# Statistics, bias rows, a PSUM bank and paces in a two-layer attention and convolution kernel

## The chip, the cores and the metric

The kernel runs on one core of a Trainium2 chip. A core has TensorE (PE, matrix products; PEld is its loading of weights), VectorE (DVE), ScalarE (ACT), GpSimd (POOL) and SyncE (SP, here only issuing DMAs), which run beside one another and wait for each other by semaphores. SBUF is the working memory; PSUM holds the results of TensorE[...]. Time is measured on the device in microseconds (us); less is better. Before the change it was 2578.98 us, the median of three runs from 2576.24 to 2585.12.

## What is computed

Two layers on x of 2 x 56 x 56 positions with 384 channels, all in float32. Layer 0 is neighbourhood attention with an MLP; layer 1 is a depthwise convolution with four scans and an MLP.

```python
# layer 0
h = neighborhood_attention(layer_norm(x, ln1_g, ln1_b), w_qkv, b_qkv, rpb, w_proj, b_proj, 12, 7)
x = x + h                                   # x1
y = layer_norm(x, ln2_g, ln2_b)
x = x + gelu(y @ w1 + b1) @ w2 + b2         # x2; w1 is 384 x 1536, w2 is 1536 x 384
# layer 1
p = layer_norm(x, n1_g, n1_b) @ w_in + b_in           # 768 channels
local = depthwise_conv3x3(p, k_conv)
mixed = 0.25 * (lr + rl + tb + bt) + local            # four exponential scans of local
x = x + (layer_norm(mixed, on_g, on_b) @ w_out + b_out)     # x3
x = x + gelu(layer_norm(x, n2_g, n2_b) @ w1 + b1) @ w2 + b2
```

## The kernel before

All 6272 tokens are worked in tiles of 128 and groups of four tiles. The order in which each engine gets its instructions is the order of the program text: it is written by hand[...].

1. Attention, up to about 669 us. It writes x1 to DRAM.
2. MLP of layer 0, groups 0 (one tile) to 12 (`groups`). While group g is in the MLP, the group before it, `waiting`, is normalised and goes through `project_in` (w_in), whose result p is stored to DRAM. Groups 1 to 4 (`EARLY`) use products with fewer multiplications: `hidden_by_seven` (block sums of w1 and of the input, so that seven products do the work of eight) and `tokens_by_seven`. Group 5 uses the first of the two; from group 6 on the plain forms `hidden` and `tokens` run.
3. Convolution and scans, from about 1015 to 1917 us. This is side work for VectorE, ScalarE and DMAs beside TensorE's products. The class `Beside` plans it: `go(worth, own)` is called after every piece of main work, adds `rate * worth - own` to a budget and issues side steps (each with its own estimate in us) until the budget is used up. `MLP` is worth 2.6, `OUT` 3.9, `ROW` 7.8; `own` counts VectorE's statistics in that piece. `until(job)` issues all steps up to a job at once. `Band` jobs do the taps (L1304) and horizontal scans (L1250, L1254), `Columns` jobs the vertical scans, with turning copies on ACT (L1352, L1370). Results are added to `mix_d` in DRAM by POOL's accumulating DMAs (L1323).
4. Layer 1's out projection and MLP, groups `dgroups`. `project_out` is called once for group 0 and then in each iteration of the loop over the first three groups (`switch = 3`), where the plain products run; from there on the seven-product forms come back with other PSUM pools (`open_banks`) and weight sums, called the switch below.

Names that matter here:

- `Norm.add` is VectorE's statistics of one tile (L221, L222), `close` (L226, and POOL's power L229) and `shift` (L250) turn them into scale and offset, `apply_by_scalar` (L257) applies them on ACT. `close_by_pool` (L236 to L239) is the form in which POOL also makes the offset.
- `statistics_ahead` (L1547 to L1565) loads tiles of x1 two by two and measures them for the groups from 6 on; each `next(statistics)` is one pair.
- `hidden_by_seven` makes for each of three units u the block sums L1670 (needed before TensorE may go on accumulating in `z[u]`) and, later, L1642. Its argument `measuring` is advanced twice in each unit: here it is the generator `both()`, which in each advance runs `ahead_of(m)` and `behind(m)` for two values of m. So what is written for m = 0 and 1 comes after the first product into `z[0]`, m = 2 and 3 before L1670 of unit 0, m = 4 and 5 in unit 1, and so on.
- `add_row` (L1136) adds a bias row to all tiles of a group by an accumulating DMA that POOL issues. `seeded` (L1225) copies the residual with its bias into a PSUM bank before `tokens` accumulates onto it.
- `bank()` hands out two PSUM banks in turn, `y_end` and `y`. `ps_t` has three banks, used in turn for transposes (`tp`) and for measuring (`xi`, L1440); `ps_m` has three for the MLP.
- `sums_of_w1` (L1591) makes five differences of blocks of w1: on POOL for layer 0, on VectorE at the switch for layer 1, where the first three go into a tile in the place of w_in.

Of the kernel before, what the change touches and what calls it, by code (L numbers as in the profile page):

```python
# [33 lines left out]
F32 = mybir.dt.float32  # L34
AF = mybir.ActivationFunctionType
ALU = mybir.AluOpType
# [6 lines left out]
P = 128  # L43
# [70 lines left out]
class Beside:  # L114
# [2 lines left out]

    def __init__(self):
        self.jobs, self.due, self.finished, self.idle = [], 0.0, set(), True
        self.late, self.rate, self.begun = [], 1.03, False  # L120
        self.steps = self.run()

    def behind(self, kind=object):
# [55 lines left out]
def block_kernel(ctx: ExitStack, tc: tile.TileContext, ins: dict, out: bass.AP):  # L179
# [914 lines left out]
    def passes(xs, xn, w1, w2, between=lambda ps: None):  # L1094
# [116 lines left out]
        def tokens(lhs, w, k, ps=None, onto=None):  # L1211

            ps = onto if onto is not None else bank() if ps is None else ps
            for m, t in enumerate(lhs):
                nc.tensor.matmul(  # L1215
                    ps, lhsT=t[:, k * P : (k + 1) * P], rhs=w[:, m, :],
                    start=m == 0 and onto is None, stop=m == len(lhs) - 1,
                    skip_group_check=onto is not None,
                )
            return ps  # L1220
# [251 lines left out]
                return 2 * STATS  # L1472
            return 0.0

        def project_out(g, mx, x, inner, then=lambda k: None):
            n = dgroups[g][1]
            x3 = io.tile([P, NT, C], F32, name="xc")
            norm = Norm(sm)
            for k in range(n):
                ps = tokens([mx[:, c, :] for c in range(NI)], w_out, k)  # L1480
                nc.vector.scalar_tensor_tensor(
                    x3[:, k, :], ps, inner.rs[:, k : k + 1], x[:, k, :], ALU.mult, ALU.add
                )
                norm.add(k, [x3[:, k, :]])
                then(k)
                beside.go(OUT, 2 * STATS)
            norm.close(n)
            return x3, norm
# [88 lines left out]
            for k in tiles:  # L1577
                yield from measure_by_vector(ahead[0], ahead[2], k)

        def sums_of_w1(w1, three, engine=nc.gpsimd):  # L1580

            h = HID // 2
            b11, b12 = w1[:, 0, :h], w1[:, 0, h:]
            b21, b22 = w1[:, 1, :h], w1[:, 1, h:]
            t1, t2, t3 = (three[:, c, :] for c in range(NC))
            t4, other = (tp.tile([P, h], F32, name=x) for x in ("w1_t4", "w1_other"))
            for to, x, y in (
                (t1, b12, b11), (t2, b22, t1), (t3, b22, b12), (t4, b21, t2),
                (other, w1[:, 2, :h], w1[:, 2, h:]),
            ):  # L1590
                engine.tensor_tensor(to, x, y, ALU.subtract)  # L1591
            return t1, t2, t3, t4, other

        def sums_of_input(hT):

# [180 lines left out]
        ps_y, ps_u, bank_b, banks_b = open_banks(fctx, "first")  # L1776
        ps_t = ps_m = ps_u
        tag = "uz"
        w1_sums = sums_of_w1(w1, tp.tile([P, NC, HID // 2], F32, name="w1_t"))
        x = xs.pop(0)  # L1780
        hT = channels(xn, groups[0][1], "L0_conv_ln2_g", "L0_conv_ln2_b")
        add_row(x, groups[0][1], "b2_0")
# [1 line left out]
        for g, (t0, n) in enumerate(groups):  # L1784
# [19 lines left out]
            if g == last:  # L1804
                beside.until((0, NI - 1))
                load_row(0, "b2_1")
                ahead = load_mix(0)
                beside.rate = 1.03
            if g < last:
                x_next, n_next = xs.pop(g + 1), groups[g + 1][1]  # L1810
                norm_next = Norm(sm) if g < EARLY.stop else Ready(g + 1)
# [22 lines left out]
            def behind(m):  # L1834

                nonlocal xn_next
                if g < last:
                    if g < EARLY.stop and 2 * m < n_next:
                        for k in range(2 * m, min(2 * m + 2, n_next)):
                            norm_next.add(k, [x_next[:, k, :]])  # L1840
                    if g < EARLY.stop and m == 1:
                        norm_next.close(n_next)
                    if g < EARLY.stop and m == 5:
                        norm_next.shift(n_next)
                    to = 7 if g < EARLY.stop else 8
                    if m == to:
                        xn_next = xp.tile([P, NT, C], F32, name="xn")
                    if to <= m < to + n_next:
                        norm_next.apply_by_scalar(m - to, x_next, xn_next)
                if m == 2 and g:  # L1850
                    add_row(x, n, "b2_0")

            def both():
                for m in range(NHID):
                    ahead_of(m)
                    behind(m)
                    if m % 2 == 0 and m > 2 and sum_steps:
                        sum_steps.pop(0)()
                    if m % 2 == 1:
                        if g > 1:  # L1860
                            next(statistics, None)
                        yield

            if early or half_early:
                s12 = [tp.tile([P, NHID // 2, MT // 2], F32, name=x) for x in ("s1", "s2")] if early else None
                low, high, finish = hidden_by_seven(
                    hT, xsums, w1, w1_sums, s12, both(), "L0_conv_b1"
                )
                hT_w = io.tile([P, NC, MT], F32, name="hT")
                nw = groups[waiting[0]][1]  # L1870
                to_channels(
                    None, [xn_w[:, k, :] for k in range(nw)], hT_w, NC, *n1,
                    banks=[
                        ps_y.tile([P, MT], F32, name="turn", tag="y"), y_end_wide,
                        ps_u.tile([P, MT], F32, name="turn", tag="ua", bufs=1),
                    ],
                )
                if half_early:
                    finish()
                    hid = [t[:, i] for t in (*low, *high) for i in range(2)]  # L1880
                    begin_convolution()
                    seeds = [seeded(x, k) for k in range(2)]
                    project_in(waiting[0], hT_w)
                else:
                    project_in(waiting[0], hT_w, finish, 0)
            else:
                for m in range(NHID):
                    next(preparing, None)
                    ahead_of(m)
                    hid.append(hidden(w1, m, hT, n, "L0_conv_b1"))  # L1890
                    behind(m)
                    if g > EARLY.stop and m in (8, 10):
                        seeds.append(seeded(x, m // 2 - 4))
                    own = STATS if m == 1 else 0.0
                    if g == last:
                        own = measure_beside(m, 0, ahead)
                    beside.go(MLP, own)
                for _ in preparing:
                    pass
                if g == 0:  # L1900
                    between(bank())
                if waiting is not None:
                    project_in(waiting[0], hT_w)
            if g == last:
                ahead[2].close(dgroups[0][1])
                w1, w2_1, w_parts = weights(1)
                for part in w_parts[:3]:
                    part()
# [67 lines left out]
        add_row(x3, dgroups[0][1], "b2_1")  # L1976
        for g, (t0, n) in enumerate(dgroups[:switch]):
            hid = []
            for m in range(NHID):
                hid.append(hidden(w1, m, hT, n, "L1_conv_b1"))  # L1980
                beside.go(MLP, measure_beside(m, g + 1, ahead))
            res = x3
            x3, norm = project_out(g + 1, *ahead)
            ahead = load_mix(g + 2)
            seeds = [seeded(res, k) for k in range(2)]
            for k in range(n):
                if g == switch - 1 and k == 2:

                    beside.until((1, NI - 1))
                    cctx.close()  # L1990
                    tp = pctx.enter_context(tc.tile_pool(name="tail", bufs=1, reuse_waits="tile"))
                    three = wp.tile([P, NC, INNER], F32, name="w1_t", tag="w_in")
                    w1_sums = sums_of_w1(w1, three, nc.vector)
                    w2_sums, sum_steps = sums_of_w2(w2, nc.vector)
                if k == n - 1:
                    hT = channels(xn, dgroups[g + 1][1], *n2)
                ps = tokens(hid, w2, k, onto=seeds.pop(0))
                if k == 0:
                    norm.shift(dgroups[g + 1][1])
                if k == n - 3:  # L2000
                    xn = normalized(norm, x3, dgroups[g + 1][1])
                beside.go(ROW)
                if k == n - 1:
                    add_row(x3, dgroups[g + 1][1], "b2_1")
                o = res[:, k, :]
                nc.scalar.copy(o, ps)
                nc.sync.dma_start(out=yout[t0 + k * P : t0 + (k + 1) * P, :], in_=o)
                if k + 2 < n:
                    seeds.append(seeded(res, k + 2))
# [146 lines left out]
```

## Time and profile before

One execution was profiled: it took 2580.42 us, of which the profile's span is 2578.6 us. TensorE's mean granted clock was 0.995.

| stage (us from the span's start) | TensorE | VectorE | ScalarE | POOL | DMA share |
|---|---|---|---|---|---|
| 835 to 855, MLP of layer 0, group 3 | 15.91 | 11.43 | 10.73 | 6.04 | 0.61 |
| 1415 to 1435, group 10 | 15.59 | 11.88 | 13.47 | 0.00 | 0.45 |
| 1640 to 1660, project_out of group 0 | 17.43 | 19.41 | 6.58 | 2.15 | 0.44 |
| 1656 to 1920, layer 1 up to the switch | 262.56 | 238.60 | 139.98 | 39.07 | 0.78 |
| 1915 to 1935, the switch | 15.32 | 19.70 | 8.90 | 9.17 | 0.91 |

The numbers are us of busy time of each engine in that stretch; a stretch of 20 us with TensorE at 15.91 has 4.09 us in which TensorE did nothing. In the first, second and last of them TensorE's granted clock was 0.83, 0.83 and 0.91, elsewhere 1.00.

### The profile page before, as it was taken

How to read it: one execution, taken by the hardware profiler on the slowest of the kernel's cores; microseconds unless marked ns; L12 is line 12 of the kernel's file. 1: busy time of each engine (PE TensorE's matmuls, PEld its weight loads, DVE VectorE, ACT ScalarE, POOL GpSimd, SP SyncE). 2: the span in 40 equal slices, each digit the busy share in tenths (PEclk: the TensorE clock that was granted, in tenths of full speed). 3: DMA queues.
4: the chain of work that ended last, by engine and by line, in shares of the span. 5: the costliest groups of instructions: out<-in, count | busy, mean ns of one | idle time of the engine just before them, and what ended most of it. 6: DMA issues, size and time to landing. Idle time of an engine off the chain costs nothing. (4 is left out here: it accounts for less than half of the span.)

```text
span 2578.6 us, 41862 instructions
## 1 busy us (share of the span) xinstructions
PE 2537.1 (98%) x16678; PEld 1737.8 (67%) x16678; DVE 1978.9 (77%) x3718; ACT 1123.9 (44%) x2033; POOL 569.0 (22%) x615
## 2 busy tenths in 40 slices
PE   9999999999999999999999999999999999999999
PEld 5666666666688777455445555555558888888888
DVE  4888978887454453799999898799897877878871
ACT  5665655655443444334444443323762233333222
POOL 0111211111542231110110011011133333333332
PEclk9999999999999999999999999999999999999999
DMA  7423454225521322657677566776881333333210
GB/s 229 152 88 98 159 179 155 83 90 192 145 67 57 86 68 63 171 169 217 174 221 265 191 187 187 246 207 151 235 202 46 74 74 74 74 74 74 47 28 21
DMA packets 155596, 342.96 MB, mean 133 GB/s; under 512 B 11158, under 2 KB 109696, under 8 KB 153088
## 3 DMA queue, kind: packets, MB, share of 16 engines
q1 hardware_dynamic: 124096, 255.65, 29.2%
q0 software_dynamic: 26352, 57.81, 13.2%
q10 hardware_dynamic: 4944, 26.74, 3.1%
q8 instruction: 133, 2.18, 0.4%
q14 instruction: 71, 0.58, 0.1%
HBM read 176.39 MB, written 134.88 MB: 121 GB/s over the span
## 5 line engine op out<-in xcount | busy, mean ns | idle before, releaser
L1304 DVE SCALAR_TENSOR_TENSOR loc<-pt,taps,loc 128x1045 f32<-128x1045 f32 (+17 forms) x288 | 366.7, 1273 | 22.0 <-ACT loc L1287 14.2
L1197 PE MATMUL mm<-hT,w 128*128 128x512 f32 x720 | 317.7, 596 | 1.2 <-ACT hT L274 1.2
L573 ACT ACTIVATE pts<-pts 119x448 f32<-119x448 f32 (+5 forms) x396 | 210.7, 573 | 109.2 <-DVE pts L563 100.0
L563 DVE TENSOR_TENSOR pts<-sc,bias 119x448 f32<-119x448 f32 (+5 forms) x396 | 219.0, 615 | 45.4 <-PE sc L552 45.0
L1197 PEld LDWEIGHTS mm<-hT,w 128*128 128x128 f32 x720 | 135.3, 191 | 162.8 <-issue 155.9
L1180 DVE STREAM_TRANSPOSE hT<-xn 32x96 f32<-32x96 f32 x784 | 211.3, 269 | 27.7 <-ACT xn L257 17.5
L406 PE MATMUL ps<-hT,wqkv 128*128 128x448 f32 x504 | 204.8, 550 | 2.1 <-ACT vs L451 1.5
L1452 DVE STREAM_TRANSPOSE turned<-mx 32x192 f32<-32x192 f32 x528 | 194.8, 369 | 6.9
L1215 PE MATMUL y<-w,hid 128*128 128x384 f32 x552 | 181.9, 486 | 0.0
L1215 PE MATMUL y_end<-w,hid 128*128 128x384 f32 x552 | 181.8, 486 | 0.0
L1215 PEld LDWEIGHTS y_end<-w,hid 128*128 128x128 f32 x552 | 104.5, 190 | 71.8
L1215 PEld LDWEIGHTS y<-w,hid 128*128 128x128 f32 x552 | 104.3, 190 | 71.5 <-issue 0.5
L1208 ACT ACTIVATE hid<-mm,chan 128x512 f32<-128x512 f32 x120 | 82.3, 686 | 156.7 <-PE mm L1197 156.7
L406 PEld LDWEIGHTS ps<-hT,wqkv 128*128 128x128 f32 x504 | 91.3, 189 | 84.3 <-issue 74.2
L1197 PE MATMUL mm<-hT,w_in 128*128 128x512 f32 x324 | 140.8, 593 | 0.6 <-DVE hid_u L1642 0.6
L229 POOL TENSOR_TENSOR rs<-rs,mhalf 128x4 f32<-128x4 f32 (+4 forms) x60 | 58.8, 981 | 314.5 <-DVE rs L226 305.5
L1623 PE MATMUL ua<-hT,w 128*128 128x256 f32 x504 | 123.7, 382 | 0.0
L1323 POOL DMA_DIRECT2D mix_d<-both x36 | 32.7, 908 | 408.4 <-ACT both L1319 326.2
L552 PEld LDWEIGHTS sc<-qT,kT 32*100 32x100 f32 (+3 forms) x3168 | 87.8, 169 | 46.6 <-DVE sum L582 7.6
L592 PE MATMUL o<-pts,vt 100*32 100x112 f32 (+3 forms) x3168 | 116.8, 264 | 0.6 <-ACT pts L573 0.6
L1630 ACT ACTIVATE hid<-hid_u,chan 128x256 f32<-128x256 f32 x168 | 76.1, 500 | 86.4 <-DVE hid_u L1642 68.8
L1197 PEld LDWEIGHTS mm<-hT,w_in 128*128 128x128 f32 x324 | 61.2, 190 | 77.5 <-issue 73.1
(207 smaller groups left out, 4985.4 us busy)
## 6 DMA issues: line engine op xcount, KB each, us to landing
loc<-loc_d SPq DMA_DIRECT2D x24, 784.0 KB
xa<-x_d SPq DMA_DIRECT2D x24, 768.0 KB
xa<-rows POOLq DMA_DIRECT2D x24, 768.0 KB, 9.3
bias<-in_bias_t ACTq DMA_DIRECT2D x13, 1344.0 KB
p_d<-mx SPq DMA_DIRECT2D x11, 1536.0 KB
mx<-mix_d SPq DMA_DIRECT2D x11, 1536.0 KB
v_d<-vs SPq DMA_DIRECT2D x49, 192.0 KB
xr<-in_x SPq DMA_DIRECT2D x49, 192.0 KB
```

Of the source, the lines that this page charges most:

```text
L406: nc.tensor.matmul(ps, lhsT=wqkv[:, c, m * P : (m + 1) * P], rhs=hT[:, c, half_of(n)], start=c == 0, stop=c == NC - 1,)
L552: nc.tensor.matmul(sc[i // 2][: w.keys, i % 2, q : q + TT], lhsT=kT[d, hg, w.keys_at + r * w.kc : w.keys_at + (r + w.rows) * w.kc], rhs=qT ...
L563: nc.vector.tensor_tensor(self.pts[:n, h : h + 2, lo:hi, :], sc[half][:n, :, at * TT : (at + hi - lo) * TT].rearrange("p h (c q) -> p h c ...
L573: nc.scalar.activation(t, t, AF.Exp)
L592: nc.tensor.matmul(o[i * HD : (i + 1) * HD, self.slot, :TT], lhsT=w.vt[:n, c, h * HD : (h + 1) * HD], rhs=self.pts[:n, i, c, :], start=c = ...
L1180: nc.vector.transpose(hT[j : j + HD, :, k * P + i : k * P + i + HD], xn[i : i + HD, k, :].rearrange("p (c q) -> p c q", c=NC)[:, :, j : j ...
L1197: nc.tensor.matmul(ps[:, : n * P], lhsT=w[:, c, m * P : (m + 1) * P], rhs=hT[:, c, : n * P], start=c == 0, stop=c == NC - 1,)
L1208: nc.scalar.activation(t[:, : n * P], ps[:, : n * P], AF.Gelu, bias=col(b1, m))
L1215: nc.tensor.matmul(ps, lhsT=t[:, k * P : (k + 1) * P], rhs=w[:, m, :], start=m == 0 and onto is None, stop=m == len(lhs) - 1, skip_group_c ...
L1304: nc.vector.scalar_tensor_tensor(to, pt[:, lo + dy - self.top : hi + dy - self.top, xt : xt + n], self.tap(dy, dx), to, ALU.mult, ALU.add,)
L1452: nc.vector.transpose(t[j : j + HD].rearrange("p (m c) -> p m c", m=NI)[:, :, i : i + HD], mx[i : i + HD, :, k * P + j : k * P + j + HD],)
L1623: nc.tensor.matmul(bank[:, i, :], lhsT=w[:, m * P : (m + 1) * P], rhs=x, start=start and i == 0, stop=True, skip_group_check=True,)
```

## The change

- `Beside.rate` is 1.04 instead of 1.03 from the start, and 1.06 instead of 1.03 from the last group of layer 0 on.
- `project_out`, called without `then`, takes the bank for every third tile (k = 2 of four) from `ps_t` instead of from `bank()`.
- The five sums of w1 are split: `sums_of_w1` makes three, always on POOL, and `more_of_w1` the other two. For layer 1, POOL makes its three at the start of the loop's group 1; VectorE makes the other two at the switch, where it made all five.
- In groups 0 to 4 the statistics of the next group's x1 come two tiles at m = 3 and two at m = 5 instead of four at m = 0 and 1; close, shift and applies follow (m = 5, 7 and 8 instead of 1, 5 and 7). The pairs of `statistics_ahead` are taken at m = 1, 7, 9 and 11 from group 1 on, instead of at every odd m from group 2 on.
- The bias row b2_0 is added to the next group's tiles after `project_in`, instead of to the group's own tiles at m = 2.

```diff
-        self.late, self.rate, self.begun = [], 1.03, False
+        self.late, self.rate, self.begun = [], 1.04, False
...
-        def project_out(g, mx, x, inner, then=lambda k: None):
+        def project_out(g, mx, x, inner, then=None):
...
-                ps = tokens([mx[:, c, :] for c in range(NI)], w_out, k)
+                third = then is None and k % 3 == 2
+                ps = tokens(
+                    [mx[:, c, :] for c in range(NI)], w_out, k,
+                    ps_t.tile([P, C], F32, name="y", tag="pt") if third else None,
+                )
...
-                then(k)
+                if then is not None:
+                    then(k)
...
-        def sums_of_w1(w1, three, engine=nc.gpsimd):
+        def sums_of_w1(w1, three):
             h = HID // 2
             b11, b12 = w1[:, 0, :h], w1[:, 0, h:]
-            b21, b22 = w1[:, 1, :h], w1[:, 1, h:]
+            b22 = w1[:, 1, h:]
             t1, t2, t3 = (three[:, c, :] for c in range(NC))
+            for to, x, y in ((t1, b12, b11), (t2, b22, t1), (t3, b22, b12)):
+                nc.gpsimd.tensor_tensor(to, x, y, ALU.subtract)
+            return t1, t2, t3
+
+        def more_of_w1(w1, sums, engine=nc.gpsimd):
+            h = HID // 2
             t4, other = (tp.tile([P, h], F32, name=x) for x in ("w1_t4", "w1_other"))
             for to, x, y in (
-                (t1, b12, b11), (t2, b22, t1), (t3, b22, b12), (t4, b21, t2),
-                (other, w1[:, 2, :h], w1[:, 2, h:]),
+                (t4, w1[:, 1, :h], sums[1]), (other, w1[:, 2, :h], w1[:, 2, h:]),
             ):
                 engine.tensor_tensor(to, x, y, ALU.subtract)
-            return t1, t2, t3, t4, other
+            return *sums, t4, other
...
-                beside.rate = 1.03
+                beside.rate = 1.06
...
-                    if g < EARLY.stop and 2 * m < n_next:
-                        for k in range(2 * m, min(2 * m + 2, n_next)):
+                    if g < EARLY.stop and m in (3, 5):
+                        for k in range(m - 3, min(m - 1, n_next)):
                             norm_next.add(k, [x_next[:, k, :]])
-                    if g < EARLY.stop and m == 1:
+                    if g < EARLY.stop and m == 5:
                         norm_next.close(n_next)
-                    if g < EARLY.stop and m == 5:
+                    if g < EARLY.stop and m == 7:
                         norm_next.shift(n_next)
-                    to = 7 if g < EARLY.stop else 8
-                    if m == to:
+                    if m == 8:
                         xn_next = xp.tile([P, NT, C], F32, name="xn")
-                    if to <= m < to + n_next:
-                        norm_next.apply_by_scalar(m - to, x_next, xn_next)
-                if m == 2 and g:
-                    add_row(x, n, "b2_0")
+                    if 8 <= m < 8 + n_next:
+                        norm_next.apply_by_scalar(m - 8, x_next, xn_next)
...
                     if m % 2 == 1:
-                        if g > 1:
+                        if m not in (3, 5):
                             next(statistics, None)
...
                     project_in(waiting[0], hT_w)
+            if g < last:
+                add_row(x_next, n_next, "b2_0")
...
         for g, (t0, n) in enumerate(dgroups[:switch]):
             hid = []
+            if g == 1:
+                three = sums_of_w1(
+                    w1, wp.tile([P, NC, INNER], F32, name="w1_t", tag="w_in")
+                )
...
-                    three = wp.tile([P, NC, INNER], F32, name="w1_t", tag="w_in")
-                    w1_sums = sums_of_w1(w1, three, nc.vector)
+                    w1_sums = more_of_w1(w1, three, nc.vector)
```

More of the change, by code (lines that the diff above doesn't have):

```diff
@@ L1778, in passes @@
         tag = "uz"
-        w1_sums = sums_of_w1(w1, tp.tile([P, NC, HID // 2], F32, name="w1_t"))
+        w1_sums = more_of_w1(w1, sums_of_w1(w1, tp.tile([P, NC, HID // 2], F32, name="w1_t")))
         x = xs.pop(0)
```

## The prediction

> **What bounds the kernel now.** I read the busy shares first, then the waits of TensorE, then the timeline at each place where TensorE stood still.
>
> ```profile
> PE 2537.1 (98%) x16678; PEld 1737.8 (67%) x16678; DVE 1978.9 (77%) x3718; ACT 1123.9 (44%) x2033; POOL 569.0 (22%) x615
> DVE  4888978887454453799999898799897877878871
> PEclk9999999999999999999999999999999999999999
> ```
>
> TensorE is busy for 98% of the span, and no edit removes a matmul. So a gain can only come from its idle time: 2578.6 - 2537.1 = 41.5 us, plus what slow clocks cost. VectorE (DVE) is at 9 tenths in slices 17 to 30, the convolution: there it is nearly a second bound.
>
> ```profile
> PE uz L1623 <- DVE sh L250: 7.8, 3, 4.1
> PE tp L271 <- ACT xn L257: 4.7, 2, 4.4
> ...
> PE yb L1229 <- ACT hT L274: 2.7, 1, 2.7
> PE y L1215 <- DVE xc L1481: 2.6, 1, 2.6
> ...
> PE ub L1623 <- issue: 2.0, 1, 2.0
> ```
>
> These five rows (us in all, times, longest) are 19.8 us and touch the edits; the rest of the idle time lies in the attention stage and at the two ends, where nothing is edited. In order of time:
>
> ```profile
> 835.35 0.56 DVE L221 BATCH_NORM_STATS2 st<-xa 128x6 f32<-128x384 f32 x1 [4.43 <-DMA xa<-x_d]
> 840.96 0.66 DVE L1670 TENSOR_TENSOR hid_u<-uz,hid_u 128x512 f32<-128x512 f32 x1
> 841.77 2.04 PE L1623 MATMUL uz<-xsums,w 128*128 128x256 f32 x4 [4.09 <-DVE sh L250]
> 843.60 1.91 PE L1623 MATMUL uz<-hT,w 128*128 128x256 f32 x4
> ...
> 1405.28 1.33 POOL L1136 DMA_DIRECT2D xa<-rows  x1
> 1419.84 0.48 ACT L1225 COPY y<-xa 128x384 f32<-128x384 f32 x1 [6.00 <-DMA xa<-rows]
> 1422.40 2.18 PE L271 MATMUL tp<-ident,xn 128*128 128x128 f32 x9 [4.41 <-ACT xn L257]
> ...
> 1648.11 4.14 PE L1215 MATMUL y<-w_out,mx 128*128 128x384 f32 x12 [2.57 <-DVE xc L1481]
> 1656.21 0.61 DVE L1481 SCALAR_TENSOR_TENSOR xc<-y,rs,xa 128x384 f32<-128x384 f32 x1
> ...
> 1916.88 3.17 ACT L1370 ACTIVATE mixed<-line 128x392 f32<-128x392 f32 x4 [3.84 <-DVE line L1254]
> 1922.42 0.32 PE L1229 MATMUL yb<-zeros 128*128 128x384 bf16 x1 [2.69 <-ACT hT L274]
> 1930.48 0.58 ACT L1662 COPY hid_u<-ub 128x512 f32<-128x512 f32 x1 [4.76 <-DMA mix_d<-mixed]
> ```
>
> (Start, length, engine, line; in brackets the idle time before and its releaser.) A, group 3: DVE waits for x1, then does four statistics and two pairs for later groups before the block sum L1670 that TensorE needs. B, group 10: ACT waits for the bias row that POOL issued late. C: the third product of project_out waits for the first to be read. E: the side work's last scan ends late, ACT's reads of it stand before the next stage's evictions, and a transfer holds the memory that the new stage's first sum needs.
>
> [...] after the 4.09 us gap four records take 1.91 us against 1.03 elsewhere. From 841.77 to 849.07 is 7.30 us; the same work one group later takes 4.56, so 2.7 us are lost besides. After 4.41 us the loads of weights stand 0.86 apart instead of 0.43 for 5.4 us: 2.7 again. After 2.69 us it costs some 1.5; after 2.57 and 2.46 nothing. [...]
>
> ```profile
> 663.95 1.80 POOL L1591 TENSOR_TENSOR w_t<-w 128x768 f32<-128x768 f32 x1
> 664.01 1.75 DVE L250 SCALAR_TENSOR_TENSOR sh<-mv,rs 128x1 f32<-128x1 f32 x1 [1.96 <-POOL rs L229]
> ```
>
> A DVE instruction on one column takes 1.75 us beside POOL, against 0.16 elsewhere.
>
> **The change, part by part.** Against the profiled run.
>
> *Statistics (A).* The gaps on `uz` are 1.26, 4.09 and 2.45 us in groups 2 to 4, with 2.7 of slow clock and a follower of 0.28: 10.8. Before the first L1670, DVE now has one pair for later groups and two tiles of x1, each tile 0.53 + 0.18: 2.9 us instead of 5.8. In the tightest group, 3, x1 lands at 835.35, so L1670 begins at 835.35 + 1.45 = 836.8 and ends at 837.5; TensorE asks at 837.68. In groups 2 and 4 over 2 us are left. All 10.8 goes. What is late next: the normalisation moves one step down, so in groups 1 to 4 the last step on ACT has one more apply of 0.70 us before the copy L1669 and the evictions L274 that release project_in. ACT has 0.29 us free there and TensorE 0.05; I take 0.3 each, 1.2 in all (ends 0 and 4 x 0.7 = 2.8). In group 4 POOL's power of 4.80 us now comes late; its successors have over 20 us. Net gain 9.6.
>
> *Bias rows (B).* The 1.3 us issue leaves POOL's queue at m == 2, where it stood behind L238 (which waits for DVE), and goes behind project_in: some 50 us before the seeds read it, for a landing of 9.3 us (14.5 at 1405). It waits there for applies that ACT has done, and behind it stand only powers of the next group. It costs nothing, and ACT's 6.00 us go: gain 4.41 + 2.7 = 7.1. Late next is L238's own chain, which feeds an apply at 1405.41 with 0.07 us to spare; pace 1.04 puts 3.5 us more side work ahead of it. ACT has some 1.3 us free per step and TensorE three banks: I take 0 (end 1).
>
> *Third bank (C).* TensorE runs on at 1645.5. But the bank comes from the three of the transposes that follow, and the third of those needs it back: it is read at 1656.21 + 0.61, by DVE, which is full there. Project_in starts at 1657.4 as before. Gain 0.1 (ends 0 and, if the buffers fall otherwise, 2.5). Its use is in the next three calls: the first product may be read 3.9 us later.
>
> *Paces.* Walking the planner with its own costs at both paces: at the switch 3.6 us of side work are left at 1.03 and none at 1.06; priced at the trace's durations, DVE is given 4.2 us more ahead of the first statistics of the second layer's group 1, and 7.1 ahead of its group 2. It has idle time for part: in this stage it waited 2.4 us at 1694 and 3.4 and 4.3 us at 1899 and 1857 for ACT copies that now come earlier in ACT's order. The gap of 1.17 us at 1674 (an eviction behind such a copy) should mostly close: 0.8.
>
> *Sums of w1.* DVE is spared 3 x 0.95 = 2.8 us at the switch; POOL gets 3 x 1.80 at 1754, with 10 us free before its next issue. But [...] 5.4 us fall on DVE. Together with the pace it is late at the first statistics by 4.2 + 5.4 - 2.4 - 0.5 (a wait at 1716) = 6.7 us. The second pair's transposes reuse that bank: read until 1769.9, wanted at 1773.5, so 3.6 are free and TensorE stands 3.1 us (ends 0 and, with slow clock, 5.8).
>
> *Switch (E).* Gaps 2.69 and 1.99 and slow clock 1.5: 6.2. Both hang on the end of the last scan at 1916.84. Against TensorE it moves by +5.4 (POOL) - 2.9 (idle already counted) - 3.1 (TensorE's own stall), and by what it recovers of 3.6 and 8.8 us of idle time after 1769; a third of that gives -4.7. Gain 4.5 (ends 0 and 6.2). DVE's next block sum ends at 1936.06 and is spared 2.8 besides, so it isn't late next.
>
> Sum: 9.6 + 7.1 + 0.1 + 0.8 - 3.1 + 4.5 = 19.0. The profiled run took 2580.42, 1.4 above the median: 2561.4 there, **2560** for the median.
>
> **The rivals.**
> - All of it lands: no stall from POOL, C in full, E in full: 10.8 + 7.1 + 2.5 + 0.8 + 6.2 = 27.4, 2551.6. For it: DVE's waits of 4.3 and 3.4 us are for ACT alone. Against: the exclusion seen at 664.
> - DVE takes back: E brings nothing, the 5.8 falls twice and ACT costs 2.8: 8.0 + 7.1 - 11.6 = 3.5, 2575.5. For it: DVE is busy 238.6 of 264 us from 1656 on. Against: it waits for TensorE four times near 1780 to 1805.
> - x1 lands later than at 835.35 and group 3 keeps its gap: 19.0 - 6.8 = 12.2, 2566.8. For it: 0.2 us of room. Against: 4.4 us in the other groups.
> - Slower: DVE is never caught up in the second layer, and each pair of statistics there finds its bank unread. The point is a lateness of about 5.5 us (one pair every 5.8 us). [...] Against: the free 25 us of VectorE.
>
> **How the numbers follow.** Forecast 0.55, all lands 0.17, taken back 0.15, late landing 0.06, slower 0.07. The forecast's own range is 2554 to 2567; half of the first rival and most of the second come in with 2551 to 2573. What a measurement can tell here is 0.3%, 7.7 us: faster 0.55 + 0.17 + 0.06 and 0.04 of the second rival, 0.82; same 0.11; slower 0.07.
>
> **What would show it.** No wait on `uz` for L250 in groups 2 to 4, and a short one of project_in for L274 there. No 6 us wait of ACT for `xa<-rows`. At project_out 0 the wait moves from `y` to `tp`. A wait on `xi` near 1773 with DVE instructions stretched beside POOL L1591. The last scan 4 to 5 us nearer to the switch's start. I am wrong if DVE's lateness reaches several pairs, or if new ACT collisions from the shifted copies outweigh the closed one.

## The result and the profile after

The changed kernel takes 2569.35 us (median; 2563.81 to 2572.71), against 2580.1 us of the kernel before beside it: a ratio of 0.9959, interval 0.9947 to 0.9970. It is faster by 10.8 us, 0.41%, where 19.0 us were forecast. The profiled execution took 2569.35 us as well, its span 2567.6 us. The time lies just outside the forecast's own range of 2554 to 2567, on the side of the rival in which VectorE takes back (2575.5).

The same two rows of the page, busy shares and VectorE's slices, for the changed kernel:

```profile
PE 2532.3 (99%) x16676; PEld 1733.0 (67%) x16678; DVE 1986.1 (77%) x3715; ACT 1124.0 (44%) x2033; POOL 570.3 (22%) x618
...
DVE  3888878887554453899999996999877877878862
```

TensorE's idle time fell from 41.5 to 35.3 us. VectorE is busy 7.2 us longer, though three sums have left it: instructions of it that now run beside POOL are stretched. In layer 0 these are five of L250, which take 1.21 to 2.58 us (6.7 us more in all, and TensorE waits for none of them); in the second layer they are taps and a scan, shown below. The waits of TensorE in the changed kernel (us in all, times, longest); line numbers from `Beside` on are those of the new file, so L1481 is now L1485 and L1591 is L1592:

```profile
PE xi L1440 <- DVE st L221: 6.7, 2, 4.2
...
PE tp L271 <- DVE xc L1485: 2.5, 1, 2.5
...
PE uz L1197 <- ACT hT L274: 1.6, 4, 0.9
PE y L1215 <- DVE xc L1485: 1.5, 1, 1.5
...
PE y_end L1215 <- ACT y_end L1225: 1.4, 1, 1.4
```

The row `uz L1623 <- DVE sh` (7.8 us before) is gone, as are the 4.4 us at `tp <- ACT xn` and the two waits at the switch. What stands there now is in the second layer: two waits of the measuring transposes `xi` for VectorE's statistics, two at the first project_out, one for a seed.

To see where the gain is lost, the table takes the start of the same TensorE instruction in both traces as a mark, and gives the length of each stage between marks (us). The first mark is the product of one column that TensorE makes at the end of group 0, at 680.93 before and 680.72 after; the rows' times are those of the kernel before.

| stage | before | after | difference | forecast |
|---|---|---|---|---|
| 681 to 1010, MLP with block sums | 328.58 | 317.36 | -11.22 | A, -9.6 |
| 1010 to 1339, groups 6 to 9 | 329.37 | 328.89 | -0.48 | 0 |
| 1339 to 1444, group 10 | 105.29 | 98.21 | -7.08 | B, -7.1 |
| 1444 to 1583 | 139.27 | 139.56 | +0.29 | 0 |
| 1583 to 1676, first project_out and project_in | 92.17 | 94.05 | +1.88 | C and D, -0.9 |
| 1676 to 1779, first pairs of statistics | 103.30 | 110.02 | +6.72 | +3.1 |
| 1779 to 1860, pairs of the next group | 81.28 | 85.75 | +4.47 | 0 |
| 1860 to 1912, last pairs and project_out | 51.63 | 53.24 | +1.61 | 0 |
| 1912 to 1953, the switch | 40.71 | 33.65 | -7.06 | E, -4.5 |
| 1953 to the end of the span | 626.07 | 626.15 | +0.08 | 0 |

The two large gains came as forecast. What was missed is VectorE's lateness between 1583 and 1912: 14.7 us, where 2.2 were forecast. Of these, 8.6 us are more idle time of TensorE, and 5.6 us are lost because its granted clock was 0.50 behind a gap (half of its busy time at that clock; called half clock below, the prediction's slow clock). The timeline of the changed kernel shows its places (start, length, engine, line; in brackets the idle time before and its releaser):

```profile
1632.27 4.14 PE L1215 MATMUL y<-w_out,mx 128*128 128x384 f32 x12 [1.51 <-DVE xc L1485]
1639.76 1.11 PE L271 MATMUL tp<-ident,xn 128*128 128x128 f32 x4 [2.48 <-DVE xc L1485]
...
1727.54 9.82 DVE L1304 SCALAR_TENSOR_TENSOR loc<-pt,taps,loc 128x616 f32<-128x616 f32 x7
1737.39 2.92 DVE L1250 TENSOR_TENSOR_SCAN both<-decay,loc 128x616 f32<-128x616 f32 x1
...
1731.88 2.61 POOL L1592 TENSOR_TENSOR w_t<-w 128x768 f32<-128x768 f32 x1
1734.57 2.20 POOL L1592 TENSOR_TENSOR w_t<-w,w_t 128x768 f32<-128x768 f32 x1
1736.73 2.29 POOL L1592 TENSOR_TENSOR w_t<-w 128x768 f32<-128x768 f32 x1
...
1760.95 0.90 PE L1440 MATMUL xi<-ident,mx 128*128 128x128 f32 x3 [4.17 <-DVE st L221]
1761.64 7.33 PE L1197 MATMUL mm<-hT,w 128*128 128x512 f32 x12
...
1843.13 3.42 DVE L1250 TENSOR_TENSOR_SCAN line<-decay,line 128x1568 f32<-128x1568 f32 x1 [1.91 <-ACT line L1352]
1846.72 1.02 DVE L221 BATCH_NORM_STATS2 st<-xi 128x6 f32<-128x384 f32 x2
1847.33 0.68 PE L1440 MATMUL xi<-ident,mx 128*128 128x128 f32 x3 [2.56 <-DVE st L221]
...
1900.24 3.42 DVE L1254 TENSOR_TENSOR_SCAN line<-decay,line 128x1568 f32<-128x1568 f32 x1
1903.70 3.21 ACT L1370 ACTIVATE mixed<-line 128x392 f32<-128x392 f32 x4 [2.08 <-DVE line L1254]
1907.26 0.48 ACT L1225 COPY y_end<-xc 128x384 f32<-128x384 f32 x1
1907.80 8.01 PE L1215 MATMUL y_end<-w,hid 128*128 128x384 f32 x24 [1.45 <-ACT y_end L1225]
```

Beside POOL's sums seven taps take 9.82 us and a scan 2.92; elsewhere in this trace seven take 6.00 and such a scan 1.44. Some 20 us later the transposes wait 4.17 us, and the twelve products behind them take 7.33 us instead of 5.3: half clock. In the next group a scan that itself waits for a turning copy of ACT stands ahead of the pair's statistics (a pair is the two statistics instructions of one tile). At the end ACT's copies of the last scan stand ahead of a seed, for which TensorE waits 1.45 us. TensorE's granted clock (the third figure from the end of each line of the view by windows, a mean over the window, idle time included) shows that the waits cost more than their length:

```profile
1637.00:1647.00 10.00, 7.53 (x20) 3.79 (x19) 9.32 (x12) 3.26 (x5) 1.17 (x2) 0.83 0.96 318
...
1757.00:1765.00 8.00, 4.05 (x7) 2.04 (x8) 7.79 (x13) 0.45 (x1) 0.89 (x1) 0.62 0.63 161
```

### The profile page after: what moved, and what is told of

It reads as the page before. It is cut to its first block, busy times and chain, and to the rows that moved or that the text cites. A ratio compares the mean times of both kernels' runs of the same rounds, so it can differ in the third digit from the quotient of the medians.

```text
span 2567.6 us, 41855 instructions
## 1 busy us (share of the span) xinstructions
PE 2532.3 (99%) x16676; PEld 1733.0 (67%) x16678; DVE 1986.1 (77%) x3715; ACT 1124.0 (44%) x2033; POOL 570.3 (22%) x618
```

## The experiments

The theory to be tried: POOL's sums and the paces together make VectorE late, each for a part. Its rivals: the pace alone; the third bank; the new places of the statistics themselves. Each run is shown in one table, as the difference of each stage's length from the kernel before (us, between the same marks); the first stage is -11.2 in all of them, and the stages from 1010 to 1583 together are -7.3 in all. So what follows concerns the rest.

Two cautions. One execution of each kernel was profiled, and whether a gap of some 2.5 us is followed by half clock, which costs 1.7 us, differs between executions (e8 and e2 in the last section): a difference of that size in a stage with such a gap is not by itself an effect of the edit. And the part ahead of the first mark, which no experiment touches, is left out of "all": it took from some 678 to 686 us in the twelve profiled executions. The medians hold this scatter too, so they tell less than the stages.

| kernel | 1583 to 1676 | to 1779 | to 1860 | to 1912 | switch | to the end | all |
|---|---|---|---|---|---|---|---|
| changed kernel | +1.88 | +6.72 | +4.47 | +1.61 | -7.06 | +0.08 | -10.79 |
| e1, sums by VectorE | +2.04 | 0.00 | +4.92 | +1.62 | -7.10 | +0.01 | -16.98 |
| e2, paces 1.03 | -0.30 | +1.38 | 0.00 | -0.01 | -0.55 | -0.02 | -18.02 |
| e3, third bank not in the first call | +3.59 | +7.77 | +4.48 | +1.62 | -7.05 | +8.42 | +0.36 |
| e4, the three together undone | -0.10 | 0.00 | 0.00 | 0.00 | +0.86 | +8.45 | -9.30 |
| e5, sums by VectorE and paces 1.03 | -0.29 | 0.00 | 0.00 | 0.00 | +1.14 | +0.07 | -17.60 |
| e6, e5 with a bank of the MLP | -2.85 | 0.00 | 0.00 | 0.00 | -0.01 | +0.02 | -21.35 |
| e7, e6 with pace 1.15 late | -2.85 | +0.01 | 0.00 | -0.01 | -3.75 | +0.04 | -25.08 |
| e8, e2 with six sums | +1.40 | +7.35 | 0.00 | 0.00 | +1.14 | +0.05 | -8.58 |
| e9, e7 with pace 1.30 | -2.85 | 0.00 | 0.00 | +5.09 | -5.41 | -0.01 | -21.70 |
| e10, e7 with POOL's sums in group 2 | -2.85 | +0.01 | +4.35 | 0.00 | -4.60 | +0.04 | -21.58 |

**e1.** The five sums of w1 by VectorE at the switch, as before.

```diff
...
-            if g == 1:
-                three = sums_of_w1(
-                    w1, wp.tile([P, NC, INNER], F32, name="w1_t", tag="w_in")
-                )
...
-                    w1_sums = more_of_w1(w1, three, nc.vector)
+                    three = wp.tile([P, NC, INNER], F32, name="w1_t", tag="w_in")
+                    w1_sums = more_of_w1(w1, sums_of_w1(w1, three, nc.vector), nc.vector)
```

> The changed kernel, with all five sums of w1 made by VectorE at the switch as before. Theory of the lock (the three POOL sums cost VectorE 5.4 us and make it late at the statistics of the second layer): the gaps on xi of 4.17 and 2.56 us shrink to under 1.5 us together, 8 to 11 us come back in that stage, and 2 to 4 us are lost at the switch, where VectorE has 2.8 us more to do: 2560 to 2565 us. Rival (the pace alone makes it late): the gaps on xi stay above 2 us each and the time is 2569 to 2573 us.

It took 2566.03 us (ratio to before 0.9946, 0.9930 to 0.9962). The first gap on `xi` vanished, with its half clock: 6.72 us. The second did not, it grew from 2.56 to 3.29 us. And nothing came back at the switch: 2.8 us more of VectorE's work there cost nothing. So the lock (VectorE's instructions take longer beside POOL's sums, 5.3 us in all in the changed kernel) is needed for the first stall, and not for the second. The expectation held for the first gap only.

**e2.** Both paces at 1.03.

```diff
-        self.late, self.rate, self.begun = [], 1.04, False
+        self.late, self.rate, self.begun = [], 1.03, False
...
-                beside.rate = 1.06
+                beside.rate = 1.03
```

> The changed kernel with both paces at 1.03. Theory of the lock: VectorE is late by some 4 us less at the first statistics, so the first gap on xi falls from 4.17 us to about 0 to 1 and the second from 2.56 us to under 1, but 3.6 us of side work are left for the switch, where 3 to 6 us come back as idle time: 2562 to 2568 us. Rival (the pace alone): both gaps vanish and the switch stays closed, 2558 us. Rival (neither matters; the third bank or the bias rows moved it): both gaps stay, 2569 us.

2565.81 us (0.9945, 0.9929 to 0.9962). The first gap on `xi` fell to 1.16 us and the second went, so the second is the pace's; but the switch kept its two gaps (2.69 and 2.00 us). So the closed switch belongs to the pace, not to the sums. The half clock at the first project_out went too, but that is not shown to be the pace's doing: e8 is the same kernel up to there, has the same gap of 2.59 us, and lost 1.7 us. The lock can be read here without the pace. Timeline of e2:

```profile
1739.32 2.59 POOL L1592 TENSOR_TENSOR w_t<-w 128x768 f32<-128x768 f32 x1
1741.99 3.05 POOL L1592 TENSOR_TENSOR w_t<-w,w_t 128x768 f32<-128x768 f32 x1
1745.00 2.35 POOL L1592 TENSOR_TENSOR w_t<-w 128x768 f32<-128x768 f32 x1
...
1739.96 2.00 DVE L1252 SCALAR_TENSOR_TENSOR both<-both 128x11 f32<-128x11 f32 x1
1743.35 9.80 DVE L1304 SCALAR_TENSOR_TENSOR loc<-pt,taps,loc 128x605 f32<-128x605 f32 x8
...
1842.83 1.00 DVE L221 BATCH_NORM_STATS2 st<-xi 128x6 f32<-128x384 f32 x2
1848.41 3.42 DVE L1250 TENSOR_TENSOR_SCAN line<-decay,line 128x1568 f32<-128x1568 f32 x1 [4.34 <-ACT line L1352]
```

The same work without POOL beside it, in e4:

```profile
1724.67 6.86 DVE L1304 SCALAR_TENSOR_TENSOR loc<-pt,taps,loc 128x605 f32<-128x605 f32 x8
...
1733.05 0.18 DVE L1252 SCALAR_TENSOR_TENSOR both<-both 128x11 f32<-128x11 f32 x1
```

2.94 and 1.82 us: the three sums cost VectorE 4.8 us here, 5.3 in the changed kernel. The last line of e2 explains the second stall: at 1.03 the scan that waits for ACT comes after the first two pairs; at 1.06 the planner had issued it, and the scan before it, ahead of the first pair.

**e3.** The third bank in the later calls alone.

```diff
-                third = then is None and k % 3 == 2
+                third = g > 0 and then is None and k % 3 == 2
```

> The changed kernel, in which project_out of the first group takes its third bank as before and only the later calls have the new one. Theory (the bank given away is missed at once by the transposes): the gap on tp of 2.48 us goes, the gap on y grows from 1.51 to about 2.5 us, and 1.5 to 2 us are gained there, 2567.5 us; the gaps on xi move by under 1 us. Rival (VectorE's lateness of one piece of taps makes both gaps, whatever bank is used): the sum of the two stays at 4 us, 2569.4 us.

2579.93 us (1.0002, 0.9991 to 1.0012): all of the gain gone, a miss of both theories. The gap on `y` at the first project_out is 5.30 us, against 1.51 and 2.48 us with the bank, so with pace 1.04 the third bank in the first call is worth 1.3 us of gaps (1.7 in the stage) and not a loss. And there is a cost that nobody had asked for; groups of lines of e3 from 1940 to 2480, a row of the plain products after the switch:

```profile
L1726 PE MATMUL y<-w,hid 128*128 128x192 f32 x372 | 65.0, 328 | 6.2 <-DVE xc L1485 6.2
```

Eight waits of 0.78 us, one in each later group, in a stage that is 8.4 us longer; the 2.2 us besides are not placed. Four calls with a third bank make twelve calls of `bank()`, an even number; three make thirteen, and the two banks change roles for the rest of the kernel.

**e4.** The edits of e1, e2 and e3 together.

> The changed kernel with the sums by VectorE, both paces at 1.03 and no third bank in the first project_out: what is left is the order of the statistics, the bias rows and the third bank in later calls. Theory: both gaps on xi vanish, the statistics and the bias rows keep their 19 us, and the switch has its gaps of before (2.69 and 1.99 us with 1.5 of slow clock): before minus 19 to 20, 2560 to 2562 us. Rival (the statistics' or bias rows' new places themselves make VectorE late in the second layer): a gap on xi of over 2 us stays, 2566 us or more.

2570.4 us (0.9966, 0.9956 to 0.9976). No gap on `xi`: the statistics and bias rows do not make VectorE late in the second layer. The switch has two gaps as before (2.65 and 3.08 us), and the turned banks cost 8.45 us, which is why the time is no better than the changed kernel's.

**e5.** The edits of e1 and e2, so e4 with the third bank in all calls.

> The changed kernel with the sums by VectorE and both paces at 1.03, but with the third bank in all calls of project_out; it differs from the run with three parts undone in the first call's bank alone. Theory (an odd number of calls of bank() turns the two banks round for the last stage, and eight gaps of 0.78 us follow from it): the eight gaps vanish and the time is some 8 us below that run, 2561 to 2563 us; the gap at the first project_out stays at 2.5 us, on tp. Rival (those gaps come from the sums or the pace): they stay, 2569 to 2571 us.

2562.16 us (0.9929, 0.9911 to 0.9947). The eight gaps are gone: the order of the banks is shown as their cause.

**e6.** e5, with the first call's third bank from the MLP's pool.

```diff
-                    ps_t.tile([P, C], F32, name="y", tag="pt") if third else None,
+                    (ps_t if g else ps_m).tile([P, C], F32, name="y", tag="pt" if g else "mm")
+                    if third else None,
```

> The kernel before it in this list, with the first project_out's third product in a bank of the three of the MLP's products instead of the three of the transposes. Theory (the bank is missed because the transposes want it 1.5 us later; project_in wants the other one 3.6 us later still): no gap on y, tp or mm of over 0.5 us at the first project_out, 2.3 to 2.7 us sooner than the kernel before it. Rival (VectorE is late there by itself and whatever needs its reading waits): a gap of 2 us or more on mm, no gain.

2559.23 us (0.9912, 0.9895 to 0.9930). TensorE's timeline in e6 has no bracket left at this place:

```profile
1633.54 5.97 PE L1215 MATMUL y<-w_out,mx 128*128 128x384 f32 x18
1639.35 1.47 PE L271 MATMUL tp<-ident,xn 128*128 128x128 f32 x12
1640.81 11.43 PE L1197 MATMUL mm<-hT,w_in 128*128 128x512 f32 x26
```

The stage is 2.6 us shorter than in e5: the transposes' need of the bank was the reason that the third bank brought nothing in the first call.

**e7.** e6, with the pace raised ahead of the last project_out before the switch.

```diff
             res = x3
+            if g == switch - 1:
+                beside.rate = 1.15
             x3, norm = project_out(g + 1, *ahead)
```

> The kernel before it in this list, with the pace raised to 1.15 from the last project_out before the switch on, after all pairs of statistics of that group. Theory (the pace closes the switch because the last scan ends sooner, and costs only where a pair of statistics stands behind a scan): the gaps at the switch of 2.69 and 2.0 us fall below 1 us together, no gap on xi, 4 to 7 us sooner than the kernel before it. Rival (VectorE's last scan ends when it ends, since it waits for ACT's copies; the switch closed in the changed kernel because TensorE came 12.8 us later): the gaps at the switch stay within 1 us of 4.7 us, and the time is the same within 2 us.

2558.65 us (0.9912, 0.9894 to 0.9930). No stall on the way; the 2.69 us at the switch are gone, the second gap is not. Timeline of e7:

```profile
1892.77 0.87 POOL L1323 DMA_DIRECT2D mix_d<-mixed  x1 [0.60 <-ACT xc L2019]
...
1902.59 0.58 ACT L1674 COPY hid_u<-ub 128x512 f32<-128x512 f32 x1 [4.63 <-DMA mix_d<-mixed]
...
1903.27 1.10 PE L1635 MATMUL ub<-xsums,w_t 128*128 128x256 f32 x4 [2.38 <-issue]
```

The last transfer of the side work is issued at 1892.77, and the new stage's first copy gets its memory 9.8 us later. "issue" on TensorE names nothing, but it goes on when that copy is done. The theory held for one gap of two, 3.75 us of the 4 to 7 expected; 2.1 of these are idle time, and 1.7 are half clock that e6 had and e7, with its gap of 2.38 us, did not. The medians don't show the step: both ratios are 0.9912.

**e8.** e2, with POOL's three sums made twice.

```diff
...
-            for to, x, y in ((t1, b12, b11), (t2, b22, t1), (t3, b22, b12)):
+            for to, x, y in ((t1, b12, b11), (t2, b22, t1), (t3, b22, b12)) * times:
...
-                    w1, wp.tile([P, NC, INNER], F32, name="w1_t", tag="w_in")
+                    w1, wp.tile([P, NC, INNER], F32, name="w1_t", tag="w_in"), 2
```

> The changed kernel with both paces at 1.03, in which POOL makes the three sums twice, one after the other (the same values again). Against the run with both paces at 1.03 and three sums, only POOL's work is added. Theory of the lock (VectorE stands while POOL sums): the gap on xi in group 1 grows from 1.16 us by 4 to 6 us, to 5 to 7 us, with 2.7 us of slow clock behind it, and the last scan ends 3 to 6 us later after the start of layer 1. Rival (the gap comes from the later position of other work): it stays below 2 us.

2573.68 us (0.9969, 0.9955 to 0.9983). TensorE's waits and its timeline in e8:

```profile
PE xi L1440 <- DVE st L221: 5.5, 1, 5.5
```

```profile
1763.01 0.90 PE L1440 MATMUL xi<-ident,mx 128*128 128x128 f32 x3 [5.46 <-DVE st L221]
```

From 1.16 to 5.46 us: 1.43 us of TensorE's time for each added sum, and 1.7 us of half clock more. The lock is shown by its dose. It recovered afterwards: at pace 1.03 the next group's pairs had no gap even then. Against e2 the last scan ended 6.0 us later after the start of the layer's MLP, and TensorE came to the switch 6.0 us later too, so the switch stayed open.

**e9.** e7, with a late pace of 1.30.

```diff
-                beside.rate = 1.15
+                beside.rate = 1.30
```

> The kernel with the late pace, at 1.30 instead of 1.15. Theory (the 2.38 us gap left at the switch hangs on the last accumulating DMA of the side work, issued 9.8 us before it lands; with the side steps sooner, it lands sooner): the gap falls below 0.5 us, 1.5 to 2.4 us gained, unless a pair of statistics or a reading of a bank waits: then at most 1 us lost at the last project_out. Rival (the scans wait for ACT's copies there, so that the last one ends when it did): the gap stays at 2 us or more, same time within 0.5 us.

2558.52 us (0.9925, 0.9910 to 0.9940). Both gaps at the switch went, but a seed came late by 4.93 us. TensorE's waits and ACT's timeline in e9:

```profile
PE y_end L1215 <- ACT y_end L1225: 4.9, 1, 4.9
```

```profile
1892.52 3.13 ACT L1370 ACTIVATE mixed<-line 128x392 f32<-128x392 f32 x4 [3.88 <-DVE line L1254]
...
1896.00 0.48 ACT L1225 COPY y_end<-xc 128x384 f32<-128x384 f32 x1
```

The copies of the last scan now stand ahead of the seed, and wait for it 3.88 us. It misses both expectations: the wait only changed its place.

**e10.** e7, with POOL's sums as in the change, but a group later.

```diff
-            if g == 1:
+            if g == 2:
                 three = sums_of_w1(
```

> The kernel with the late pace of 1.15, but with the three sums by POOL at the start of the loop's group 2, where VectorE waits for ACT's copies between vertical scans. Theory of the lock with cover (5 us of POOL's sums fall into waits that are there anyway): no gap on xi, and the switch is at most 1 us better, since a DMA holds it: 0 to 1 us gained. Rival (the lock shifts the scans one for one): the last scan ends 3 to 5 us later, the gaps at the switch grow by 3 to 5 us or a gap on xi of 2 to 4 us appears, 3 to 6 us slower than the kernel with the sums by VectorE.

2556.61 us (0.9922, 0.9906 to 0.9937). The cover did not hold; timeline of e10:

```profile
1815.52 1.82 POOL L1593 TENSOR_TENSOR w_t<-w,w_t 128x768 f32<-128x768 f32 x1
1817.30 4.94 POOL L1593 TENSOR_TENSOR w_t<-w 128x768 f32<-128x768 f32 x1
...
1815.56 5.07 DVE L1254 TENSOR_TENSOR_SCAN line<-decay,line 128x1568 f32<-128x1568 f32 x1
```

Both engines' instructions are stretched. The scan begins just after the second sum and takes 5.07 us instead of 3.42: it ends 3.3 us after that sum. The third sum takes 4.94 us and ends 1.6 us after the scan. So the sums did not fall into VectorE's waits. A gap on `xi` of 2.44 us with half clock costs 4.35, and 0.85 of it comes back at the switch. By the stages it is 3.5 us behind e7; the medians don't tell them apart.

## Why the prediction was half right

- **A, statistics:** right; 9.6 forecast, 11.2 measured. The three waits on `uz` went. ACT's delay came as four waits of 0.90, 0.23, 0.24 and 0.24 us, 0.9 more than before (1.2 forecast). Half clock cost 2.95 us there (from 840.8 to 847.7, of which TensorE was busy for 5.9 us) and not 2.7; some 0.9 us are not placed.
- **B, bias rows:** right; 7.1 forecast, 7.1 measured, 7.3 in the runs at 1.03. Nothing took its place: of the gaps in group 10 none is left.
- **C, third bank:** the mechanism was right, and e2 measures it: the wait moved from `y` to `tp`, and the stage gained 0.3 us (0.1 forecast). What failed beside it is that the pace was priced from the second layer on alone. At 1.04 VectorE is late at the first project_out already: 1.51 and 2.48 us of gaps instead of 2.57. Without the bank it would have been 5.30 (e3). The 1.5 us of half clock that this trace lost there besides may be chance: at 1.03, e8 lost 1.7 and e2 nothing.
- **D:** 0.8 forecast; the gap of 1.17 us went. It stands in all runs at 1.03, so the pace closed it. With it the gaps of this stage are 3.99 us in all, against 3.73 before. (The prediction's five rows leave this gap out; not all of the rest lay in the attention stage and at the two ends.)
- **POOL's lock and the pace, the step that failed by its size:** -3.1 forecast, -12.8 measured (6.72 + 4.47 + 1.61). That the three sums would hold taps and scans up for all of their 1.80 us each was an estimate, and it was right: 5.3 us on VectorE against 5.4. So was the room of 3.6: in e2 the lock of 4.8 us left a gap of 1.16. The lateness was undersized: 4.17 of gap and 3.6 of room make 7.8 instead of 6.7, and with 5.3 for the lock the pace's net share is 2.5 instead of 1.3 (an estimate from these gaps). The stage lost 2.55 us besides the gap, nearly all by half clock: this is the end of 5.8 that the prediction named and did not take. And the sum stopped at the first pair. It let VectorE catch up in its idle time, but it spends that idle time waiting for ACT's turning copies in program order: the pace moved such a scan ahead of the next group's first pair, 4.47 us, and ACT's copies of the last scans ahead of a seed, 1.61 us. This is the rival in which VectorE takes back, for the stalls, and the prediction's own sign of being wrong, lateness at several pairs, came in part: two pairs of twelve found their bank unread.
- **E, switch:** 4.5 forecast, 7.1 measured, for another reason. I reckoned with the last scan's end; what counts is its end against TensorE's arrival at the switch's mark. It ends 5.0 us after the mark before and in e2, 1.3 after in e7, and 4.1 ahead of it in the changed kernel and in e1. In the changed kernel the last scan came 3.6 us later after the start of the layer's MLP than before; TensorE, held up above, came 12.8 us later. So much of E is the stalls' own time, given back. It needs the pace as well: in e1 TensorE came 6.5 us later and the scan 2.6 sooner than before, while in e8, at 1.03, the scan came later by as much as TensorE and nothing closed. The prediction had counted TensorE's own stall in this, but at 3.1 us; and the rival "DVE takes back" had E bring nothing, where the stalls themselves bring it.
- **Half clock:** the prediction priced each gap by its length: nothing after 2.46 and 2.57 us, some 1.5 after 2.69. But after the same gap of 2.59 us e8 lost 1.7 us and e2 nothing (last section), so these prices held for the profiled execution alone.

The sum: 11.2 + 7.3 (group 10 and its neighbours) - 1.9 - 12.8 + 7.1 - 0.1 = 10.8 us. Errors of both signs meet in it: A and E brought 4.2 us more than forecast, C, D and the lock with the pace 12.5 us less.

e7 beats both kernels: 0.9912 of the kernel before (0.9894 to 0.9930), against 0.9959 (0.9947 to 0.9970) of the changed one; by the stages it is 14.3 us ahead, but its profiled execution had no half clock from 681 us to the last products (mean granted clock 1.00 over its span), where the changed kernel's lost 5.6 us to it. It keeps A, B and the third bank, leaves the sums to VectorE, and raises the pace only where no pair of statistics is left. That the late pace adds to e6 is shown by the gap that closed, not by the medians.

Open: which of the two paces costs how much at the first project_out and in the second layer was not tried apart; 1.04 stands for the first only because 1.06 begins with the last group, so that the side work ahead of that project_out is set by both. The third bank in the later calls brought nothing at 1.03 (those stages are at 0.00 in e4 and e5); at the paces of the change it was not tried apart.

## What to carry to other kernels

A faster pace for a full engine's side work moved the waits here more than it removed them: against e2 it gained 6.5 us at the switch and lost 12 or more ahead of it. Raise it where nothing urgent stands behind the side work, and there only. Work moved to an idle engine is not free when the two slow one another, as POOL and VectorE did here (three sums cost VectorE 4.8 to 5.3 us); price it at the busy engine, and compare with leaving it there. Count the handings-out of a rotating pair of buffers when one is taken from elsewhere: an odd number turns them round for everything that follows.

## What the runs showed of the hardware

- Half clock. Between 681 us and the last products, the granted clock of the kernel before is 0.50 in three stretches, 840.83 to 847.66, 1421.10 to 1427.92 and 1922.86 to 1926.27 us, and that of the changed kernel in three, 1639.39 to 1642.80, 1758.86 to 1765.68 and 1847.60 to 1851.02 us. Each begins within a gap of TensorE or at most 0.5 us behind it: gaps of 4.09, 4.41 and 2.69 us before, of 2.48, 4.17 and 2.56 us after. With the gaps of 2.46 and 2.57 us in the kernel before, the clock stays at 1.00. e8 and e2 have the same gap of 2.59 us at the same place of the program, and only e8 has half clock there (start, end, length, TensorE's busy time, ...; the clock is third from the end), first e8, then e2:

```profile
1636.74:1640.15 3.41, 0.86 (x5) 0.69 (x6) 3.31 (x6) 1.17 (x3) 0.00 (x0) 1.00 0.88 170
1640.15:1643.56 3.41, 3.41 (x5) 1.35 (x4) 3.34 (x5) 0.61 (x1) 0.00 (x0) 0.50 0.98 345
...
1640.55:1643.97 3.42, 1.44 (x7) 0.96 (x8) 3.31 (x6) 1.19 (x2) 0.00 (x0) 1.00 0.99 215
1643.97:1647.38 3.41, 3.41 (x10) 1.50 (x9) 3.34 (x5) 0.72 (x2) 0.00 (x0) 1.00 0.99 368
```

  In e8 the 3.41 us ahead of half clock hold 2.55 us of idle time of TensorE; in e2 the first stretch holds 1.98 and the second none. The 3.41 us at half clock in e8, with TensorE busy throughout, cost 1.7 us. Why one of the two executions had it and the other did not was not shown.
- POOL and VectorE slowed one another: three sums cost VectorE 5.3 us in the changed kernel and 4.8 in e2, and the sums, 1.80 us each at 664, took 2.20 to 3.05 us beside taps and scans. In e10 the scan took 5.07 us instead of 3.42, and the third sum 4.94: the scan ends 3.3 us, about its usual length, after the sum ahead of it, and the third sum 1.6 us after that scan.
